# Segment attention with batch norm: the output stage takes its first four groups one at a time, and its matrix and vector operations in larger pieces

## The chip, the cores and the metric

The kernel runs on one core of a Trainium2 chip. The core's engines each work through their own queue: PE (TensorE, matrix products; its weight loads are shown apart as PEld), DVE (VectorE), ACT (ScalarE), POOL (GpSimd) and SP (SyncE, which here only issues transfers). Transfers are issued from the queues of SP, ACT and POOL and carried out by the core's 16 DMA engines. The metric is the device time of one execution in microseconds (us), lower is better. Times inside an execution are counted from the start of the span in the profile.

## The reference

There are N = 16384 tokens of D = 256 features and 8 segments. A token's segment is `bids`; its place in the segment is its index less the segment's start found by a binary search. Places are clamped to a padded table of 8 x 3072.

```python
q, k, v = feat @ Wq, feat @ Wk, feat @ Wv            # 32, 32 and 256 columns
starts = jnp.searchsorted(bids, jnp.arange(B))
pos = jnp.arange(N) - starts[bids]
qp, kp, vp = pad(q), pad(k), pad(v)                  # zeros(8, 3072, .).at[bids, pos].set(.)
scores = where(mask[:, None, :], einsum('bld,bmd->blm', qp, kp), -1e9)
rp = einsum('blm,bmd->bld', softmax(scores), vp)
t = rp[bids, pos] @ Wt
mu, var = t.mean(axis=0), t.var(axis=0)              # over all tokens
out = feat + relu((t - mu) / sqrt(var + 1e-5) * gamma + beta)
```

The mean and the variance need the `t` of all tokens, so nothing of the output can be finished before attention is over.

## The kernel before, in words

The segment ids of this input are not sorted, so most tokens' places fall outside their segment's table. Such a token reads one of 16 edge rows of the attention result (two per segment). Every other token has an attended row of its own: these are collected in lists, 48 tiles of 128 tokens (8 segments, 6 tiles each) in `tk`, with their features in `xs`, and a further list of 3 tiles, `L` with the features `xL`, whose rows are fetched by gathers (L836). A second, general path for other inputs (L41 to L530) isn't run here.

Attention is done segment by segment; the matrix products of L1008 and L953 fill PE. `statistics` (L1036) then forms mean, variance and scale, and the 16 finished edge rows after scale, shift and relu, split in three bf16 parts (48 rows), `y3` (L1062). It is complete at 255.35 us. What comes after is the output stage (L1405 to L1539), and it is where the change is made.

*Dense groups.* The tokens are 16 groups of 1024, each a tile of [128, 8, 256] f32 (1 MB). `ORDER` (L564) is the order in which they are treated: 0 to 6, then 15, 14, 13, 12, then 7 to 11. In this text d0 to d15 count in the order of treatment. For each group, PE multiplies a one-hot selection of edge rows `hot` by `y3` (L1483, one product per 128 tokens, 256 columns), the feature tile is added, and the tile goes to `out`. A group's parity decides which half of PE's rows it uses (rows 0 to 47 or 64 to 111), so the products of two groups of different parity can run at the same time.

*Pairs and iterations.* The groups are treated as eight pairs. A pair takes four iterations; each does two 128-token tiles of both groups, in accumulator tiles `pf` of 128x512 (one bank of the accumulator memory each; the pool `psF` has five). In the first two pairs DVE adds the features to the products (L1497), for both groups. From the third pair on it does so only for the first group of the pair; for the second, PE adds the features too, as a product with the identity matrix (L1488, f32, 256 columns, which is two passes on PE), and ACT copies the sum back into the tile (L1495).

*Buffers.* The feature tiles rotate through `IOB` = 6 buffers, `f_bufs`. Five lie in `work`, the memory of attention, and are loaded as soon as attention ends (L1083). The sixth, and then each buffer once its old group has been written, is loaded from SP's queue (L1473). The write of a group (L1501) is issued from ACT's queue after the pair, behind whatever copies ACT has in front of it.

*Rows.* `rows` (L1443) treats the listed tokens, two tiles at a time: on DVE multiply by `scale` (L1454), add `shift` (L1456), relu and add the features (L1458), with the intermediate `py` in accumulator memory (pool `psY`, two tiles of one bank). `scale` and `shift` come from three DVE operations behind the second pair (L1503 to L1505). `n_ops` says how many of these operations follow the additions of an iteration: none in pairs 0 and 1, 4 in 2 and 3, 3 later. `short_path_holds` (L1429) checks that no denominator has overflowed; it is called behind the fourth pair.

*Row writes.* POOL writes the finished rows to `out` with indirect transfers, one per tile, 51 in all (`put`, L1515, its transfer L1516). A listed token has also been written by its dense group, with a value that isn't its own; the row must come after that. So each write waits for dense groups, by an arm of a switch chosen from the segments' bounds (`ARMS`, L565). In this input the first six writes wait for d0 to d2, the next twelve for d0 to d4, eighteen for d0 to d6, and the last fifteen for d0 to d10 (12 tiles of `tk` and 3 of `L`).

What sets the order: DVE and PE follow the order of the Python loop, which is written out by hand (`manual_schedule`). ACT, SP and POOL are put in order by the framework's planner from its own estimates, so a group's write can stand behind copies of the next pair.

Of the kernel before, what the change touches and what calls it, by code (L numbers as in the profile page):

```python
# [18 lines left out]
P = 128  # L19
# [13 lines left out]
PART = 4  # L33
QA = TMIN * P
PB = 512
IOB = 6
LIM = 1.0e30


# [492 lines left out]
def segment_attention_bn_kernel(  # L532
# [44 lines left out]
    with ExitStack() as short:  # L577
# [828 lines left out]
        ahead = list(f_bufs)  # L1406
        while len(f_bufs) < IOB:
            f_bufs.append(io.tile([P, GT, D], F32, name=f"f{len(f_bufs)}"))
        fin = short.enter_context(tc.tile_pool(name="fin", bufs=1))
        psM = short.enter_context(tc.tile_pool(name="psM", bufs=1, space=PSUM))  # L1410
        psY = short.enter_context(tc.tile_pool(name="psY", bufs=2, space=PSUM))
        psF = short.enter_context(tc.tile_pool(name="psF", bufs=5, space=PSUM))
        out3 = out.rearrange("(g p i) d -> g p i d", p=P, i=GT)

# [9 lines left out]


        scale = psM.tile([P, 1, D], F32, name="scale")
        shift = fin.tile([P, 1, D], F32, name="shift")

        def short_path_holds():  # L1429

            lim = fin.tile([P, TT], F32, name="lim")
            nc.vector.tensor_scalar(lim, rdens, LIM, None, ALU.is_lt)
            good = fin.tile([P, TT], F32, name="good")
            odd = fin.tile([P, 1], F32, name="odd")
            nc.vector.scalar_tensor_tensor(
                good, rdens, 1.0 / LIM, lim, ALU.is_gt, ALU.mult, accum_out=odd
            )
            nc.vector.tensor_scalar(odd, odd, -1.0, float(TT), ALU.mult, ALU.add)
            ps_bad = psF.tile([P, 1], F32, tag="pf", name="ps_bad")
            nc.tensor.matmul(ps_bad, ones, odd, start=True, stop=True)  # L1440
            nc.vector.tensor_tensor(bad, ps_bad, over, ALU.add)

        def rows():  # L1443


            work = [(tk[:, ts(u, 2), :], xs[:, ts(u, 2), :]) for u in range(TT // 2)]
            for at in range(0, LT, 2):
                t = slice(at, min(at + 2, LT))
                work.append((L[:, t, :], xL[:, t, :]))
            for t, x in work:  # L1450
                T = t.shape[1]
                py = psY.tile([P, 2, D], F32, tag="py", name="py")
                p = py[:, 0:T, :]
                nc.vector.tensor_tensor(p, t, scale.to_broadcast([P, T, D]), ALU.mult)  # L1454
                yield
                nc.vector.tensor_tensor(p, p, shift.to_broadcast([P, T, D]), ALU.add)  # L1456
                yield
                nc.vector.scalar_tensor_tensor(t, p, 0.0, x, ALU.max, ALU.add)  # L1458
                yield
# [4 lines left out]
        dense = []  # L1464
        row = rows()

        pairs = [(k, k + 1) for k in range(0, NG, 2)]
        n_ops = [0, 0, 4, 4, 3, 3, 3, 3]
        with tc.manual_schedule(engines={mybir.EngineType.DVE, mybir.EngineType.PE}):
            for n, pair in enumerate(pairs):  # L1470
                for k in pair:
                    if k >= len(ahead):
                        nc.sync.dma_start(f_bufs[k % IOB], feat3[ORDER[k]])  # L1473
                for i in range(0, GT, 2):
                    pfs = {}
                    for k in pair:
                        pfs[k] = psF.tile([P, 2, D], F32, tag="pf", name=f"pf{ORDER[k]}")
                    for u in range(2):
                        for k in pair:
                            half, c = ORDER[k] % 2, ORDER[k] // 2  # L1480
                            r = slice(64 * half, 64 * half + 3 * NE)
                            on_pe = n > 1 and k % 2
                            nc.tensor.matmul(  # L1483
                                pfs[k][:, u, :], hot[r, c, i + u, :], y3[r, :],
                                start=True, stop=not on_pe,
                            )
                        if on_pe:
                            nc.tensor.matmul(  # L1488
                                pfs[k][:, u, :], ident, f_bufs[k % IOB][:, i + u, :],
                                start=False, stop=True,  # L1490
                            )
                    for k in pair:
                        two = f_bufs[k % IOB][:, i : i + 2, :]
                        if n > 1 and k % 2:
                            nc.scalar.copy(two, pfs[k])  # L1495
                        else:
                            nc.vector.tensor_add(two, two, pfs[k])  # L1497
                    for _ in range(n_ops[n]):
                        next(row, None)
                for k in pair:  # L1500
                    dense.append(nc.scalar.dma_start(out3[ORDER[k]], f_bufs[k % IOB]).ins)  # L1501
                if n == 1:
                    nc.vector.tensor_copy(scale[:, 0, :], scale_s)  # L1503
                    nc.vector.tensor_mul(shift[:, 0, :], mean, scale[:, 0, :])
                    nc.vector.tensor_sub(shift[:, 0, :], beta_bc, shift[:, 0, :])  # L1505
                if n == 3:
                    short_path_holds()
            for _ in row:
                pass
# [75 lines left out]
```

## Time and profile before

| what | us |
|---|---|
| median of 9 runs | 368.43 (364.29 to 369.02) |
| the profiled execution | 366.9 |
| its span | 365.0 |
| `y3` complete | 255.35 |
| write of d4 issued, landed | 282.04, 291.50 |
| last addition of d4 on DVE ends | 277.39 |
| write of d10 issued | 324.88 |
| last dense write landed | 353.74 |
| last row write starts, lands | 350.61, 354.72 |

Over the whole span PE is busy 288.9 us (79%), DVE 262.7 (72%), POOL 171.5 (47%) and ACT 109.3 (30%). In the output stage the dense writes take 7.2 / 8.0 / 9.7 us from issue to landing (minimum, median, maximum), and the loads of feature tiles 6.2 / 8.9 / 10.8. In one row of events the first number is the start in us, the second the length; then come engine, line and operation, the tiles written and read, and in square brackets the idle time of the engine just before, with what the profile holds to have ended it. In a table by stage, each engine has its busy time and number of instructions; then come the granted clock of PE as a share of full speed, the mean busy share of the DMA engines and what they moved in GB/s. In the list of waits each line has an engine, its tile and line, who released it, the time in total, how often, and the longest.

### The profile page before, as it was taken

How to read it: one execution, taken by the hardware profiler on the slowest of the kernel's cores; microseconds unless marked ns; L12 is line 12 of the kernel's file. 1: busy time of each engine (PE TensorE's matmuls, PEld its weight loads, DVE VectorE, ACT ScalarE, POOL GpSimd, SP SyncE). 2: the span in 40 equal slices, each digit the busy share in tenths (PEclk: the TensorE clock that was granted, in tenths of full speed). 3: DMA queues.
4: the chain of work that ended last, by engine and by line, in shares of the span. 5: the costliest groups of instructions: out<-in, count | busy, mean ns of one | idle time of the engine just before them, and what ended most of it. 6: DMA issues, size and time to landing. Idle time of an engine off the chain costs nothing. (4 is left out here: it accounts for less than half of the span.)

```text
span 365.0 us, 4145 instructions
## 1 busy us (share of the span) xinstructions
PE 288.9 (79%) x1139; PEld 178.5 (49%) x1139; DVE 262.7 (72%) x776; ACT 109.3 (30%) x208; POOL 171.5 (47%) x181
## 2 busy tenths in 40 slices
PE   1577599696899899399989999992896879999700
PEld 0335466473586488056865786661242334433200
DVE  7985399899798635488994356567998968888500
ACT  8525534233424441333222615430011102211100
POOL 3343353778782600477787710010305177776740
PEclk9998879898999999659999999997555555555555
DMA  4011111214013202211242010569699999996560
GB/s 114 24 32 30 38 56 33 66 39 139 0 49 123 70 9 63 62 48 44 72 127 69 10 59 29 177 216 370 262 392 381 407 398 379 351 407 263 201 234 3
DMA packets 20905, 53.34 MB, mean 146 GB/s; under 512 B 6606, under 2 KB 13344, under 8 KB 16746
## 3 DMA queue, kind: packets, MB, share of 16 engines
q1 hardware_dynamic: 11493, 25.06, 19.6%
q10 hardware_dynamic: 2421, 16.83, 11.2%
q0 software_dynamic: 6928, 10.81, 9.9%
q14 instruction: 48, 0.39, 0.4%
q8 instruction: 15, 0.25, 0.3%
HBM read 26.67 MB, written 29.92 MB: 155 GB/s over the span
## 5 line engine op out<-in xcount | busy, mean ns | idle before, releaser
L1008 PE MATMUL po<-work 128*128 128x257 f32 x394 | 100.5, 403 | 7.4 <-ACT work L972 4.4
L1008 PEld LDWEIGHTS po<-work 128*128 128x128 f32 x394 | 76.6, 201 | 23.9 <-ACT work L972 7.5
L836 POOL DMA_INDIRECT xs<-in_r_feat,idx x48 | 52.7, 1099 | 50.3 <-issue 27.6
L1516 POOL DMA_INDIRECT out<-tk,idx x48 | 47.3, 985 | 37.3 <-DVE py L1454 15.3
L836 POOL DMA_INDIRECT reads_r<-reads_of,idx x48 | 53.6, 1116 | 20.2 <-issue 14.7
L1488 PE MATMUL pf<-work,ident 128*128 128x256 f32 x64 | 39.1, 714 | 3.0 <-DMA work<-in_r_feat 3.0
L953 PE MATMUL pv<-wvt,work 128*128 128x256 f32 x164 | 37.9, 383 | 1.2 <-ACT work L945 1.0
L972 ACT ACTIVATE work<-s,mask 128x512 f32<-128x512 f32 (+2 forms) x62 | 32.6, 601 | 13.3 <-PE s L967 10.8
L953 PEld LDWEIGHTS pv<-wvt,work 128*128 128x128 f32 x164 | 30.6, 190 | 8.7 <-ACT work L945 3.0
L1483 PE MATMUL pf<-y,hot 48*128 48x256 bf16 x128 | 27.0, 391 | 9.8 <-DVE y L1062 7.1
L1497 DVE TENSOR_TENSOR work<-work,pf 128x512 f32<-128x512 f32 x40 | 26.1, 682 | 10.9 <-PE pf L1483 10.9
L997 ACT ACTIVATE sq<-tk 128x256 f32<-128x256 f32 x39 | 16.3, 417 | 55.4 <-DVE tk L1013 51.1
L1483 PEld LDWEIGHTS <-hot 48*128 48x128 bf16 x128 | 7.0, 104 | 43.4 <-issue 43.3
L967 PE MATMUL s<-work 32*128 32x512 f32 (+2 forms) x124 | 25.9, 607 | 2.7 <-ACT work L972 2.7
L1012 DVE RECIPROCAL rdens<-po 128x1 f32<-128x1 f32 x39 | 6.1, 160 | 26.6 <-PE po L1008 26.5
L922 PE MATMUL px<-ident,xs 128*128 128x128 f32 x82 | 17.5, 319 | 7.9 <-issue 2.6
L1495 ACT COPY work<-pf 128x512 f32<-128x512 f32 x16 | 9.4, 586 | 47.6 <-PE pf L1488 47.6
L934 PE MATMUL pqk<-work,wqk 128*128 128x512 f32 (+2 forms) x52 | 21.9, 561 | 0.2 <-ACT work L927 0.2
L1488 PEld LDWEIGHTS pf<-work,ident 128*128 128x128 f32 x64 | 16.0, 310 | 12.4 <-issue 9.1
L922 PEld LDWEIGHTS px<-ident,xs 128*128 128x128 f32 x82 | 10.7, 159 | 19.3 <-issue 6.6
L957 ACT COPY work<-pv 128x512 f32<-128x512 f32 (+1 forms) x21 | 12.1, 576 | 25.8 <-PE pv L953 25.8
L1488 PE MATMUL pf<-f,ident 128*128 128x256 f32 x32 | 19.5, 714 | 0.0
(241 smaller groups left out, 380.9 us busy)
## 6 DMA issues: line engine op xcount, KB each, us to landing
work<-in_r_feat SPq DMA_DIRECT2D x14, 1024.0 KB, 8.4
out<-work ACTq DMA_DIRECT2D x14, 1024.0 KB, 7.9
t_rows<-tk SPq DMA_DIRECT2D x3, 768.0 KB, 3.9
t_rows<-tk SPq DMA_DIRECT2D x4, 512.0 KB, 5.0
f<-in_r_feat SPq DMA_DIRECT2D x2, 1024.0 KB, 6.2
out<-f ACTq DMA_DIRECT2D x2, 1024.0 KB, 8.5
eb<-edge_of SPq DMA_DIRECT2D x16, 96.0 KB, 2.4
t_rows<-tk SPq DMA_DIRECT2D x4, 256.0 KB, 3.1
```

The costliest lines, as they stand in the source:

```text
L836: nc.gpsimd.indirect_dma_start(out=dst, out_offset=None, in_=table, in_offset=bass.IndirectOffsetOnAxis(ap=ind, axis=0), bounds_check=n - ...
L922: nc.tensor.transpose(px[:, ts(t, P)], xs[:, b * FT + t0 + t, ts(h, P)], ident)
L934: nc.tensor.matmul(pqk[:, 0:w], wqk[:, h, :], xT[:, h, own_c], start=(h == 0), stop=(h == DH - 1),)
L953: nc.tensor.matmul(pv[:, t, :], xT[:, h, ts(t0 + t, P)], wvt[:, h, :], start=(h == 0), stop=(h == DH - 1),)
L967: nc.tensor.matmul(s[:, i, 0:w], k[g, t // 4, :], q[g, c : c + w], start=True, stop=True)
L972: nc.scalar.activation((pr_b if c else pr_a)[:, t, 0:w], s[:, i, 0:w], AF.Exp, bias=mask[:, m : m + 1],)
L997: nc.scalar.activation(sq, tk[:, at, :], AF.Square)
L1008: nc.tensor.matmul(po, pr[:, t, ts(r, P)], v[:, t, :], start=(t == 0), stop=(t == T - 1))
L1483: nc.tensor.matmul(pfs[k][:, u, :], hot[r, c, i + u, :], y3[r, :], start=True, stop=not on_pe,)
L1488: nc.tensor.matmul(pfs[k][:, u, :], ident, f_bufs[k % IOB][:, i + u, :], start=False, stop=True,)
L1497: nc.vector.tensor_add(two, two, pfs[k])
L1516: w = nc.gpsimd.indirect_dma_start(out=out, out_offset=bass.IndirectOffsetOnAxis(ap=idx[:, at : at + 1], axis=0), in_=y, in_offset=None, b ...
```

## The change

- The first four groups are treated one by one; the other twelve as six pairs. All additions of the first four stay on DVE, as before.
- `scale` and `shift` are computed behind the third group (d2), and the first unit of rows follows at once; the second unit follows behind d3.
- In a pair, the identity product takes 512 columns (both tiles of an iteration) and comes first; the one-hot products are then added to it.
- Rows go four tiles at a time (128x1024; the 3 tiles of `L` in one piece), so there are 13 units of three operations instead of 26. `py` is one tile of two banks instead of two of one. `n_ops` becomes 2 in the first two pairs and 1 later.
- There are seven feature buffers instead of six. To make room, `shift` and the small tiles of `short_path_holds` move into `late`, memory that `statistics` has finished with. `short_path_holds` is called behind the second pair, (6, 7).

```diff
@@ -33,7 +33,7 @@
 PART = 4
 QA = TMIN * P
 PB = 512
-IOB = 6
+IOB = 7
 LIM = 1.0e30
 
 
@@ -1406,9 +1406,8 @@
         ahead = list(f_bufs)
         while len(f_bufs) < IOB:
             f_bufs.append(io.tile([P, GT, D], F32, name=f"f{len(f_bufs)}"))
-        fin = short.enter_context(tc.tile_pool(name="fin", bufs=1))
         psM = short.enter_context(tc.tile_pool(name="psM", bufs=1, space=PSUM))
-        psY = short.enter_context(tc.tile_pool(name="psY", bufs=2, space=PSUM))
+        psY = short.enter_context(tc.tile_pool(name="psY", bufs=1, space=PSUM))
         psF = short.enter_context(tc.tile_pool(name="psF", bufs=5, space=PSUM))
         out3 = out.rearrange("(g p i) d -> g p i d", p=P, i=GT)
 
@@ -1424,14 +1423,14 @@
 
 
         scale = psM.tile([P, 1, D], F32, name="scale")
-        shift = fin.tile([P, 1, D], F32, name="shift")
+        left = late.rearrange("p t m -> p (t m)")
+        shift = left[:, 0:D].unsqueeze(1)
 
         def short_path_holds():
 
-            lim = fin.tile([P, TT], F32, name="lim")
+            lim, good = (left[:, D + i * TT : D + (i + 1) * TT] for i in range(2))
+            odd = left[:, D + 2 * TT : D + 2 * TT + 1]
             nc.vector.tensor_scalar(lim, rdens, LIM, None, ALU.is_lt)
-            good = fin.tile([P, TT], F32, name="good")
-            odd = fin.tile([P, 1], F32, name="odd")
             nc.vector.scalar_tensor_tensor(
                 good, rdens, 1.0 / LIM, lim, ALU.is_gt, ALU.mult, accum_out=odd
             )
@@ -1443,13 +1442,10 @@
         def rows():
 
 
-            work = [(tk[:, ts(u, 2), :], xs[:, ts(u, 2), :]) for u in range(TT // 2)]
-            for at in range(0, LT, 2):
-                t = slice(at, min(at + 2, LT))
-                work.append((L[:, t, :], xL[:, t, :]))
-            for t, x in work:
+            work = [(tk[:, ts(u, 4), :], xs[:, ts(u, 4), :]) for u in range(TT // 4)]
+            for t, x in [*work, (L, xL)]:
                 T = t.shape[1]
-                py = psY.tile([P, 2, D], F32, tag="py", name="py")
+                py = psY.tile([P, 4, D], F32, tag="py", name="py")
                 p = py[:, 0:T, :]
                 nc.vector.tensor_tensor(p, t, scale.to_broadcast([P, T, D]), ALU.mult)
                 yield
@@ -1464,46 +1460,54 @@
         dense = []
         row = rows()
 
-        pairs = [(k, k + 1) for k in range(0, NG, 2)]
-        n_ops = [0, 0, 4, 4, 3, 3, 3, 3]
+
+
+        steps = [(0,), (1,), (2,), (3,), (4, 5), (6, 7), (8, 9), (10, 11), (12, 13), (14, 15)]
+        n_ops = [0, 0, 0, 0, 2, 2, 1, 1, 1, 1]
+
+        def feats(k):
+            if k >= len(ahead):
+                nc.sync.dma_start(f_bufs[k % IOB], feat3[ORDER[k]])
+
         with tc.manual_schedule(engines={mybir.EngineType.DVE, mybir.EngineType.PE}):
-            for n, pair in enumerate(pairs):
-                for k in pair:
-                    if k >= len(ahead):
-                        nc.sync.dma_start(f_bufs[k % IOB], feat3[ORDER[k]])
+            for n, step in enumerate(steps):
+                for k in step:
+                    feats(k)
                 for i in range(0, GT, 2):
                     pfs = {}
-                    for k in pair:
+                    for k in step:
                         pfs[k] = psF.tile([P, 2, D], F32, tag="pf", name=f"pf{ORDER[k]}")
+                        if k != step[0]:
+                            nc.tensor.matmul(
+                                pfs[k], ident, f_bufs[k % IOB][:, i : i + 2, :],
+                                start=True, stop=False,
+                            )
                     for u in range(2):
-                        for k in pair:
+                        for k in step:
                             half, c = ORDER[k] % 2, ORDER[k] // 2
                             r = slice(64 * half, 64 * half + 3 * NE)
-                            on_pe = n > 1 and k % 2
                             nc.tensor.matmul(
                                 pfs[k][:, u, :], hot[r, c, i + u, :], y3[r, :],
-                                start=True, stop=not on_pe,
+                                start=(k == step[0]), stop=(k == step[0] or u == 1),
                             )
-                        if on_pe:
-                            nc.tensor.matmul(
-                                pfs[k][:, u, :], ident, f_bufs[k % IOB][:, i + u, :],
-                                start=False, stop=True,
-                            )
-                    for k in pair:
+                    for k in step:
                         two = f_bufs[k % IOB][:, i : i + 2, :]
-                        if n > 1 and k % 2:
+                        if k != step[0]:
                             nc.scalar.copy(two, pfs[k])
                         else:
                             nc.vector.tensor_add(two, two, pfs[k])
                     for _ in range(n_ops[n]):
                         next(row, None)
-                for k in pair:
+                for k in step:
                     dense.append(nc.scalar.dma_start(out3[ORDER[k]], f_bufs[k % IOB]).ins)
-                if n == 1:
+                if n == 2:
                     nc.vector.tensor_copy(scale[:, 0, :], scale_s)
                     nc.vector.tensor_mul(shift[:, 0, :], mean, scale[:, 0, :])
                     nc.vector.tensor_sub(shift[:, 0, :], beta_bc, shift[:, 0, :])
-                if n == 3:
+                if n in (2, 3):
+                    for _ in range(3):
+                        next(row)
+                if n == 5:
                     short_path_holds()
             for _ in row:
                 pass
```

## The prediction, made before the changed kernel was run

> **What bounds the kernel now.** I read the end first and went backwards. The chain that ended last has only four pieces, all in the last 16 us: POOL's writes of rows, L1516. So the next question is what released that queue, and I read POOL's own row of events (start, length, in square brackets the idle time before and what the profile blames):
>
> ```profile
> span 365.0 us, 4145 instructions
> PEclk9998879898999999659999999997555555555555
> 282.04 0.34 ACTq L1501 DMA_DIRECT2D out<-work  x1
> ...
> 292.36 0.99 POOL L1516 DMA_INDIRECT out<-tk,idx  x1 [8.37 <-DVE py L1456]
> 293.65 0.98 POOL L1516 DMA_INDIRECT out<-tk,idx  x1 [0.30 <-issue]
> ...
> 332.57 0.98 POOL L1516 DMA_INDIRECT out<-tk,idx  x1 [1.82 <-DVE py L1454]
> ...
> 350.61 0.99 POOL L1516 DMA_INDIRECT out<-L,idx  x1 [0.30 <-issue]
> ```
>
> There are 51 row writes. Six run at 275.77 to 284.0. Then POOL idles 8.37 us; from 292.36 a write starts every 1.29 (0.98 and 0.30), with one further wait of 1.82, which is 1.52 over the usual 0.30. The check: 44 steps x 1.29 = 56.76; 292.36 + 56.76 + 1.52 = 350.64, and the last one starts at 350.61. So the end is the start of this second batch, plus that extra wait, plus a fixed chain. The vector operations named in the brackets were long done: the 8.37 ends 0.86 after the write of the fifth dense group (d4, counted from 0 in order of treatment) landed at 291.50, and the wait at 332.57 ends about as long after the eleventh (d10, issued 324.88) landed. After the last start come 4.1 us to its landing (354.72) and 10.3 of closing work.
>
> Why does d4 land so late? Its last addition ended at 277.39, but on ACT its write stands behind a copy that waits for PE, which waited for the load of the next odd group:
>
> ```profile
> 279.24 1.22 PE L1488 MATMUL pf<-work,ident 128*128 128x256 f32 x2 [3.01 <-DMA work<-in_r_feat]
> 281.98 0.59 ACT L1495 COPY work<-pf 128x512 f32<-128x512 f32 x1 [5.45 <-PE pf L1488]
> ...
> core 0: us, PE busy (x) PEld busy (x) DVE busy (x) ACT busy (x) POOL busy (x), PEclk, DMA share, GB/s
> 255.50:266.00 10.50, 8.89 (x39) 2.83 (x40) 9.89 (x17) 0.00 (x0) 3.03 (x3) 0.50 0.71 281
> 266.00:279.00 13.00, 10.23 (x28) 4.04 (x28) 12.66 (x22) 2.35 (x4) 2.03 (x2) 0.50 1.00 395
> 279.00:294.00 15.00, 11.58 (x30) 4.74 (x30) 13.95 (x23) 2.34 (x4) 5.26 (x6) 0.50 0.99 382
> 294.00:345.00 51.00, 49.00 (x130) 19.88 (x130) 39.91 (x67) 9.07 (x16) 37.90 (x39) 0.50 0.88 338
> ...
> DVE work L1497 <- PE pf L1483: 10.9, 18, 1.6
> ```
>
> The table by stage says two more things. PE is busy 49.00 of 51.00 us after 294 and DVE waits 10.9 us for it, at a granted clock of 0.50 throughout. And DMA is full (1.00, 0.99) while d4 is on its way. Yet all of PE's work ends before the row writes do: the last dense write lands at 353.74, 1.0 before the last row. So after 292 PE has little to give: it can only take away the 1.52 for d10 and about a microsecond of crowding at the end. The price of the change is set before 292.
>
> **The change part by part** (times from the start of the span; the profiled execution took 366.9: span 365.0 and 1.9 around it. That is 1.5 below the median of 368.43 of the nine runs; I work out a difference and add it to the median.)
>
> *First four groups one by one, seventh buffer.* The 16 first additions stay on DVE. Before, they ran pair by pair, 0.60 apart, 256.11 to 265.65. Now d0, d1, d2 need 4 each and finish at about 258.6, 261.0, 263.4 (before: writes issued 260.42, 261.01, 265.20). Nothing is added; d2, on which the first six row writes wait, leaves 1.8 earlier. These six end the batch 2 to 3 us earlier, which is hidden: POOL then waits for d4 either way. The seventh buffer is one 1 MB load at 251 instead of later on SP's queue; it runs where DMA share is 0.71 and takes the load of the second odd group out of 268.39 to 279.20. With that, PE's 3.01 wait goes.
>
> *Rows four tiles at a time, scale and first two units pulled forward.* An operation of 128x512 takes 682 to 698 ns; the nearest rows for 128x1024 f32 are other vector operations on this chip at 1203 to 1229 (L1111, L1112, L1125). 39 operations of about 1.25 (dependent) or 1.13 (overlapped) replace 78 of 0.72 or 0.60: some 4 to 5 us of DVE saved over the stage, but DVE was not the bound after 294. What matters is the order at the start: scale and shift (three of 0.42) end at 264.7, unit 0 (3 x 1.25) at 268.4, the four additions of d3 at 270.9, unit 1 at 274.6. Then come the additions of d4 with two row operations between them: 0.60 + 1.25 + 1.13 = 2.98 per step, the fourth ends at 274.6 + 3 x 2.98 + 0.69 = 284.2. Before, d4 was added up at 277.39: **this part moves d4 back by 6.8 us on DVE**, of which the next paragraph shows how much was waiting anyway. Working with one accumulator tile instead of two makes a unit's first operation wait for the last one of the unit before, but both are DVE's own, in order.
>
> *Identity products of 512 columns.* Before, an iteration (two tiles of both groups of a pair) took 2.96 on PE: four identity passes of 0.575 (0.59 and 0.56) and two pairs of one-hot products at 0.33. Now: two passes of 512. Back-to-back f32 products of 257 columns at the half clock were 0.427 apart in the attention stage (158.8 to 162.4), so 512 columns are 0.853 of streaming; if the 0.148 by which the tail's passes exceed that stays with each pass, 1.00. Lower bound 2 x 0.853 + 0.66 = 2.37, upper 2 x 1.00 + 0.66 = 2.66 (and 2.96 if nothing is gained). I take 2.53, between them, since the second weight load can hide behind a longer pass.
>
> *When d4 leaves.* In the changed kernel's order on ACT, d4's write stands behind the third copy of the following pair (before: behind the first). PE's first identity is free at 264, but its iteration is completed by the one-hot product whose accumulator bank comes free with the first addition of d3 at 269.3: iteration 1 ends at 270.0. Six more of 2.53 end at 285.2; the seventh uses the bank that ACT copies out of only after the sixth, 0.8 more: 286.0. So the write goes at **286.1, against 282.04: 4.1 later**. By 2.37 it is 285.1 (DVE's 284.2 is the floor), by 2.66 it is 286.9, by 2.96 it is 288.7.
>
> *When it lands.* Before, 9.46 (282.04 to 291.50), together with two loads, d5's write and row writes. Now the first row writes are over and the load of the odd group is not there, so it shares with one load and d5's tail: nearest is d6 before, issued 291.47 beside a load at 291.57, landed after 7.23. The writes' minimum is 7.2, their median 8.0; almost alone in the beginning it was 4.65. I take 7.2: 293.3, and the second batch starts 0.87 later at **294.2, against 292.36: +1.8**. Bounds 285.1 + 6.8 (2 MB at the 395 GB/s of 266 to 279 is 5.3, and 1.5 of the first write's 4.65 for being under way) and 286.9 + 9.46, each + 0.87: 292.8 to 297.2.
>
> *What is late next.* d10: its write must land before the 31st step, 294.2 + 30 x 1.29 = 332.9. PE takes two of four pairs at 2.53 and the other at DVE's 2.98, so it leaves at 321 (before 324.88), lands at 329: **the 1.52 goes**. d6 (in the case of this input the 13th write of the batch waits for it: 294.2 + 12 x 1.29 = 309.7) leaves after pair two at some 298 and lands by 307: not late, by 2.7 us. The row units: the last ends with PE's last iteration, about 341 to 342, 6 us before the first L row. Nothing else waits. At the end the dense write is over some 3 us earlier than 353.74, so the last row lands in 3.5 to 4.1 instead of 4.1: 0 to -0.6.
>
> *The sum.* +1.8 (second batch) - 1.52 (d10) - 0.3 (last landing) = 0.0. The profiled execution would stay at 366.9, the median at 368.4. With the bounds: a batch at 292.8 gives +0.4 - 1.52 - 0.6 = -1.7, one at 297.2 gives +4.8 - 1.52 - 0 = +3.3.
>
> **Weighing a rule: PE's clock.** The tail before kept 0.50 although PE is busy 0.96 of 294 to 345: busy is not streaming. Per iteration 4 x 0.427 + 2 x 0.21 = 2.13 of 2.96 stream, 0.72; of 2.53 it would be 0.84, and in the attention stage, with products back to back, the clock row shows 9s. At full clock PE's iteration would halve; then DVE's 284.2 holds d4, it leaves at 284.4, lands at 291.2 to 291.6, the batch starts at 292.1 to 292.5.
> The Trainium skill, "TensorE: Matmul & The Clock Gate", Part 1, says that the throttled state is the default and one busy window of about 3.4 us releases it. Read simply, that rule would have freed the clock before, where the row shows 0.50 for 110 us; so the trace asks for a denser window than the page's word "busy" gives, and no row says if 0.84 is enough. By the rule the sum would be -1.7 to -2.2, by the row 0.0.
>
> **The rivals.**
> *Clock rises (faster).* As above: 292.3 + 56.76 = 349.1, 1.5 less than 350.61, less 0.3 to 0.6 at the end, and up to 1 more if d4's landing meets emptier queues: -1.8 to -3, 365.4 to 366.6. For it: 0.84 against 0.72; against: DVE-paced iterations (2.98) fall back to 0.71.
> *d4 lands as slowly as before (slower).* DMA was at 0.99, and the same megabytes pass; 286.1 + 9.46 + 0.87 = 296.4, last write at 353.2: +2.3 to +2.6, 371; with iterations of 2.96 +5, 373. It decides when the second batch starts after 292.36 + 1.52 + 1.84 = 295.7.
> *The change gains nothing on PE and hides all the same.* Iterations of 2.96 but a landing of 7.2: 288.7 + 7.2 + 0.87 = 296.8, +2.6. It joins the case above.
> *The first batch's row writes or d6 hold the queue:* d6 only if it leaves after 301; unlikely, +1 to +2.
>
> **How the numbers follow.** Even chain 0.44 (its own range 366.8 to 370.0), clock 0.26, late d4 0.26, other small waits 0.04. "Within 0.5%" is 1.84 us, about what a measurement of this kernel can tell from no change. The even case gives 0.28 within, 0.08 faster, 0.08 slower; clock 0.21 faster, 0.05 within; late d4 0.23 slower, 0.03 within; the rest 0.02 on each side. Together faster 0.31, within 0.36, slower 0.33. For 8 in 10 the range takes in the clock's full -3 and late d4 to +3.3: 365.2 to 371.7.
>
> **What would show it.** Right: d4's write issued at 285 to 287 behind a copy, POOL's long wait ending at 293 to 295, no second wait near 332, last row at 350 to 351.5; identity passes of 0.85 to 1.0; vector operations of 1024 at 1.2 to 1.25; granted clock 0.50 in the tail. Wrong: a clock above 0.5 after 265, an issue after 288, a landing above 9, a second long wait on POOL, or row writes farther apart than 1.29.

## The result, and the profile after

The changed kernel takes 364.03 us (median of 16 runs, 360.25 to 366.52) against 367.63 (53 runs of before): a ratio of 0.9883 with a 95% interval of 0.986 to 0.9906. It is 1.2% faster. I had forecast no change, with a range from 365.2 up: wrong, and on the side of the rival in which PE's clock rises. The profiled execution took 364.68, span 362.9.

The page of the changed kernel, its head, and the row of the granted clock in tenths over 40 slices:

```profile
span 362.9 us, 4009 instructions
PE 257.6 (71%) x1091; PEld 161.6 (45%) x1091; DVE 257.3 (71%) x737; ACT 109.2 (30%) x208; POOL 172.1 (47%) x181
PEclk9996989898799999959999999999557757985855
```

Before, the clock row ended in twelve fives. Now there are sevens, eights and a nine among them. The table by stage, with the stages of the prediction (the columns are busy time and number of instructions by engine, then granted clock, DMA share and GB/s):

```profile
255.50:266.00 10.50, 9.24 (x34) 3.76 (x34) 9.60 (x19) 0.00 (x0) 3.03 (x3) 0.50 1.02 424
266.00:279.00 13.00, 9.41 (x29) 2.52 (x28) 12.83 (x15) 2.45 (x5) 3.77 (x4) 0.60 0.99 389
279.00:294.00 15.00, 4.42 (x18) 1.32 (x18) 14.83 (x16) 2.23 (x4) 2.56 (x4) 0.75 1.01 408
294.00:340.00 46.00, 27.28 (x98) 8.17 (x98) 31.62 (x40) 8.80 (x15) 35.05 (x36) 0.75 0.90 341
```

PE's busy time from 279 to 294 fell from 11.58 to 4.42: it is no longer what DVE waits for there. DVE is busy 14.83 of 15.00, so DVE now holds d4. The events of ACT around d4's write, and POOL's row writes:

```profile
282.69 0.59 ACT L1496 COPY work<-pf 128x512 f32<-128x512 f32 x1 [1.57 <-PE pf L1489]
284.98 0.34 ACTq L1502 DMA_DIRECT2D out<-work  x1
...
273.63 1.03 POOL L1520 DMA_INDIRECT out<-tk,idx  x1 [8.37 <-DVE py L1450]
...
293.63 0.98 POOL L1520 DMA_INDIRECT out<-tk,idx  x1 [11.83 <-DMA out<-work]
...
332.53 0.98 POOL L1520 DMA_INDIRECT out<-tk,idx  x1 [0.55 <-issue]
...
350.57 0.98 POOL L1520 DMA_INDIRECT out<-L,idx  x1 [0.30 <-issue]
```

d4 leaves at 284.98, 0.03 after its last addition (284.27 + 0.68 on DVE); the copy ahead of it in the line of ACT was done 1.7 earlier (282.69 + 0.59). The long wait before the second batch is still there (11.83; before 8.37), the 1.82 before the 37th write (the first that needs d10) has shrunk to 0.55.

In this execution the edge rows `y3` were complete at 256.38, 1.03 later than in the profile of before. The code ahead of them is the same. The changed kernel without its row writes (below) has 256.51, two other kernels 254.77 and 255.29; whether the later start is chance, these five profiles can't say. I count from there:

| from `y3` on, us | before | forecast | after |
|---|---|---|---|
| d4's write issued | 26.69 | 30.75 | 28.60 |
| issue to landing of d4 | 9.46 | 7.2 | 7.85 |
| second batch of row writes starts | 37.01 | 38.85 | 37.25 |
| extra wait before the 37th row write | 1.52 | 0 | 0.24 |
| last row write starts | 95.26 | 95.6 | 94.19 |
| its landing takes | 4.11 | 3.8 | 2.22 |
| closing work | 10.28 | 10.28 | 10.11 |
| end of span | 109.65 | 109.7 | 106.52 |

The stage is 3.13 us shorter. Against the forecast, 1.6 of it is the second batch (DVE instead of PE holds d4) and 1.6 the landing of the last row write. Against before, the second batch is no gain (0.24 later): 1.28 come from the wait for d10, 1.89 from the last landing and 0.17 from the closing work.

### The profile page after: what moved, and what is told of

The parts are those of the page before. It is cut to its first block, busy times and chain, and to the rows that moved or that the text cites. A ratio compares the mean times of both kernels' runs of the same rounds, so it can differ in the third digit from the quotient of the medians.

```text
span 362.9 us, 4009 instructions
## 1 busy us (share of the span) xinstructions
PE 257.6 (71%) x1091; PEld 161.6 (45%) x1091; DVE 257.3 (71%) x737; ACT 109.2 (30%) x208; POOL 172.1 (47%) x181
## 4 chain that ended last, share of the span: by engine, by line
PE 40%; DVE 39%; issue 8%; DMA 4%; POOL 3%; ACT 2%; DVEq 0%; ACTq 0%; POOLq 0%
PE po L1008 19%; PE pv L953 7%; DVE work L1498 4%; PE s L967 4%; DVE py L1450 4%; PE pqk L934 4%; DVE py L1452 4%; DMA out<-tk,idx 3%; POOL out L1520 3%; PE px L922 3%; DVE tk L1454 3%; DVE tk L1013 2%; DVE work L941 2%; DVE oh L850 2%; DVE acc L998 1%
## 5 line engine op out<-in xcount | busy, mean ns | idle before, releaser
L1008 PEld LDWEIGHTS po<-work 128*128 128x128 f32 x394 | 75.7, 199 | 26.4 <-ACT work L972 7.5
L1498 DVE TENSOR_TENSOR work<-work,pf 128x512 f32<-128x512 f32 x32 | 20.6, 679 | 14.3 <-issue 10.4
L1481 PE MATMUL pf<-work,ident 128*128 128x512 f32 x32 | 21.7, 767 | 12.6 <-DMA work<-in_r_feat 10.2
L1489 PE MATMUL pf<-y,hot 48*128 48x256 bf16 x128 | 18.5, 329 | 11.8 <-DVE y L1062 7.1
L922 PE MATMUL px<-ident,xs 128*128 128x128 f32 x82 | 16.7, 310 | 9.1 <-ACT work L945 3.7
L934 PE MATMUL pqk<-work,wqk 128*128 128x512 f32 (+2 forms) x52 | 20.6, 533 | 0.4 <-ACT work L927 0.4
L993 DVE SCALAR_TENSOR_TENSOR acc<-tk,reads_r,acc 128x256 f32<-128x256 f32 x39 | 18.7, 479 | 0.9
L1013 DVE SCALAR_TENSOR_TENSOR tk<-po,rdens,sref 128x256 f32<-128x256 f32 x39 | 18.7, 481 | 0.9
```

The lines of the kernel that those rows point to most:

```text
L922: nc.tensor.transpose(px[:, ts(t, P)], xs[:, b * FT + t0 + t, ts(h, P)], ident)
L934: nc.tensor.matmul(pqk[:, 0:w], wqk[:, h, :], xT[:, h, own_c], start=(h == 0), stop=(h == DH - 1),)
L1008: nc.tensor.matmul(po, pr[:, t, ts(r, P)], v[:, t, :], start=(t == 0), stop=(t == T - 1))
L1013: nc.vector.scalar_tensor_tensor(tk[:, at, :], po[:, 0:D], rdens[:, one], sref, ALU.mult, ALU.subtract)
L1481: nc.tensor.matmul(pfs[k], ident, f_bufs[k % IOB][:, i : i + 2, :], start=True, stop=False,)
L1489: nc.tensor.matmul(pfs[k][:, u, :], hot[r, c, i + u, :], y3[r, :], start=(k == step[0]), stop=(k == step[0] or u == 1),)
```

## The experiments

Two theories. **Clock:** with the identity product first, PE streams densely enough that its clock is granted in full, and that carries the gain. **Order and buffers:** the gain comes from the first groups one by one and the seventh buffer, and the clock is beside the point.

A remark that all but the runs without row writes need: they landed on chips on which the kernel before takes 403 to 409 us (medians) instead of 368. Its own trace there is shown below. Ratios are always against runs of before on the same chip. In the profiles from there `y3` is complete anywhere between 279.1 and 294.2 us, in code that is the same in all of them; that spread is wider than what the change is worth. So I add, where it helps, how long the profiled execution took from `y3` to the end of its span: 120.5 us for before, 118.7 and 119.1 for two profiles of the changed kernel. These are single executions.

### One part undone, one part alone

The identity product of 512 columns put into the kernel before, and nothing else:

```diff
+on_pe = n > 1
+if on_pe:
+    k = pair[1]
+    nc.tensor.matmul(pfs[k], ident, f_bufs[k % IOB][:, i : i + 2, :], start=True, stop=False)
 for u in range(2):
     for k in pair:
...
-        nc.tensor.matmul(pfs[k][:, u, :], hot[r, c, i + u, :], y3[r, :], start=True, stop=not on_pe)
+        mix = on_pe and k % 2
+        nc.tensor.matmul(pfs[k][:, u, :], hot[r, c, i + u, :], y3[r, :], start=not mix, stop=(not mix or u == 1))
-    if on_pe:
-        nc.tensor.matmul(pfs[k][:, u, :], ident, f_bufs[k % IOB][:, i + u, :], start=False, stop=True)
```

> The kernel before with one part of the change: in the pairs, the identity product takes 512 columns and comes first. Clock theory: PE's iteration streams more densely, the granted clock rises to full in part of the stage after 268 us, d10 leaves earlier and the second long wait of the row writes (1.52) goes, the last dense write ends earlier: 1.5 to 2.5 us faster than before. Rival (the order of the first groups and the seventh buffer make the gain, the clock is beside the point): within 0.7 us of before.

Measured: 0.9944 (0.9903 to 0.9985), a median of 409.23 against 409.45; the clock row of the output stage has sevens and eights again. So the clock rises with this part alone. The time doesn't decide: by the ratio it is 0.6% (2.3 us of 409), as the clock theory said, but the interval goes from 0.6 to 4.0 us, and the medians differ by 0.2, as the rival said.

The reverse, the changed kernel with the products of before:

```diff
-if k != step[0]:
-    nc.tensor.matmul(pfs[k], ident, f_bufs[k % IOB][:, i : i + 2, :], start=True, stop=False)
 for u in range(2):
...
+    if len(step) > 1:
+        nc.tensor.matmul(pfs[k][:, u, :], ident, f_bufs[k % IOB][:, i + u, :], start=False, stop=True)
```

> The changed kernel with the identity products of before (256 columns, behind the one-hot product). Clock theory: granted clock 0.50 through the whole output stage, PE's iteration 2.96, d4 leaves at 288 to 289 instead of 285, the second batch of row writes starts at 296 to 298: 3 to 6 us slower than the changed kernel, so 367 to 370. Rival (order and buffers make the gain): within 1 us of the changed kernel's 364.

> The changed kernel with identity products of 256 columns, again, now beside the changed kernel on one chip. Clock theory: clock 0.50 throughout, d4 leaves 3 to 4 us later, the whole 2 to 3 per cent slower than the changed kernel and 1 to 2 per cent slower than before. Rival (order and buffers make the gain): within 0.4 per cent of the changed kernel.

> The changed kernel with identity products of 256 columns behind the one-hot products, once more on another chip. As before: clock 0.50 in the whole output stage, 1.5 to 2 per cent slower than the kernel before.

Measured: 1.0161 (1.0112 to 1.021), 1.0211 (1.0143 to 1.0278) and 1.0142 (1.0049 to 1.0234) of before, on three chips. The granted clock is 0.50 through the whole output stage in each. From `y3` to the end the first and the third took 124.2 and 126.9, against 118.7 and 119.1 for the changed kernel. On the chip of the second, the changed kernel itself stood beside it:

> The changed kernel itself, beside the others on one chip. Clock theory: granted clock above 0.5 in parts of the output stage from about 272 us on, 1 to 1.6 per cent faster than before, as on record.

Measured for the changed kernel: 1.0005 (0.9955 to 1.0055). So there its gain over before was gone, against what I expected; but 2.1% lie between it and the version with the old products. The rival's "within 0.4 per cent of the changed kernel" falls: with everything else of the change in place, the order of PE's products is worth 2%.

The order of the first groups alone (with 256 columns, rows two tiles at a time, six buffers):

```diff
-pairs = [(k, k + 1) for k in range(0, NG, 2)]
-n_ops = [0, 0, 4, 4, 3, 3, 3, 3]
+steps = [(0,), (1,), (2,), (3,), (4, 5), (6, 7), (8, 9), (10, 11), (12, 13), (14, 15)]
+n_ops = [0, 0, 0, 0, 4, 4, 2, 2, 2, 2]
...
-if n == 1:
+if n == 2:
     nc.vector.tensor_copy(scale[:, 0, :], scale_s)
...
+if n in (2, 3):
+    for _ in range(6):
+        next(row)
```

> The kernel before with one part of the change: the first four groups one by one, first rows behind the third and fourth; identity products of 256 columns, rows two tiles at a time, six buffers as before. Clock theory: clock 0.50, d4 held back on DVE to about 285 and by PE to 288, the second batch at 296 to 298, d10 in time: 2 to 5 us slower than before. Rival (the order makes the gain): 1 to 4 us faster than before.

Measured: 1.0187 (1.0124 to 1.025), clock 0.50. In its profile, of an execution of 425.7 us, the second batch starts 41.7 us after `y3` (335.93 less 294.23), against 37.5 for the kernel before on such a chip. The order of the groups, with the rows brought forward, costs time when it is alone: 7.7 us by the ratio, more than I had said; its rival expected a gain.

The changed kernel with `IOB = 6`:

> The changed kernel with six feature buffers. Clock theory: DVE holds d4 at 285 either way, the load of the seventh group comes later and PE waits for it, which costs 0 to 1.5 us. Rival (the seventh buffer carries the gain): 2 to 4 us slower than the changed kernel.

Measured: 0.9871 (0.9811 to 0.993) of before; the changed kernel wasn't on that chip. On two others of the kind it stood at 1.0005 and 1.0089, so nothing says that the seventh buffer is worth anything there. d4's write leaves 28.6 after `y3`, as it does with seven.

The changed kernel with rows two tiles at a time (`psY` with two one-bank tiles, `n_ops` doubled):

> The changed kernel with rows two tiles at a time (twice as many operations behind each iteration, two one-bank accumulator tiles). Clock theory: DVE needs 6 operations of 0.65 to 0.72 for what now takes 3 of 1.25, some 0.4 us more per unit; d4's last addition comes about 1.5 later, so 1 to 2 us slower than the changed kernel; the clock rises as it does there. Rival (the larger row operations carry the gain): 3 us slower or more, no gain left over before.

Measured: a median of 410.78 of 12 runs, beside 408.61 for the changed kernel and 408.81 for before; no ratio with an interval could be formed. The 2.2 us are close to the expectation but settle nothing. In its profile d4's write leaves 30.3 after `y3` instead of 28.6, about the 1.5 later that was expected, and the clock rises.

### The width, or the order of the products?

The changed kernel with identity products of 256 columns, but both first and in a row:

```diff
-nc.tensor.matmul(pfs[k], ident, f_bufs[k % IOB][:, i : i + 2, :], start=True, stop=False)
+for u in range(2):
+    nc.tensor.matmul(pfs[k][:, u, :], ident, f_bufs[k % IOB][:, i + u, :], start=(u == 0), stop=False)
```

> The changed kernel with identity products of 256 columns that come first, both tiles of an iteration in a row, then the four one-hot products. Does the width of 512 release the clock, or the order alone? If the width: each pass keeps its 0.15 us over the streaming, the iteration is 2.8 to 2.96, clock 0.50, like the kernel with 256 behind the one-hot products. If the order: passes 0.43 apart, iteration 2.5, the clock rises, within 0.5 per cent of the changed kernel.

By time it is unclear: 1.0103 (1.0038 to 1.0167) of before, from five runs of 399.4 to 406.49, with no changed kernel beside it. From `y3` to the end its profile took 116.5, a little less than the changed kernel's. The trace is clear on the clock. PE's events in the changed kernel, in this one, then in the one with 256 columns behind the one-hot products (its third run), all at half clock but for the last row of the first, in which the clock rises:

```profile
270.57 2.08 PE L1481 MATMUL pf<-f,ident 128*128 128x512 f32 x2
272.58 0.61 PE L1489 MATMUL pf<-y,hot 48*128 48x256 bf16 x4
273.11 2.07 PE L1481 MATMUL pf<-f,ident 128*128 128x512 f32 x2
275.66 1.46 PE L1481 MATMUL pf<-f,ident 128*128 128x512 f32 x2
```

```profile
298.71 2.07 PE L1482 MATMUL pf<-f,ident 128*128 128x256 f32 x4
300.72 0.61 PE L1490 MATMUL pf<-y,hot 48*128 48x256 bf16 x4
301.26 2.07 PE L1482 MATMUL pf<-f,ident 128*128 128x256 f32 x4
303.26 0.61 PE L1490 MATMUL pf<-y,hot 48*128 48x256 bf16 x4
```

```profile
295.97 1.22 PE L1489 MATMUL pf<-f,ident 128*128 128x256 f32 x2
297.12 0.40 PE L1484 MATMUL pf<-y,hot 48*128 48x256 bf16 x2
297.45 1.22 PE L1489 MATMUL pf<-f,ident 128*128 128x256 f32 x2
298.60 0.40 PE L1484 MATMUL pf<-y,hot 48*128 48x256 bf16 x2
```

Four passes in a row start 2.55 apart from the next four (298.71 to 301.26), with the one-hot products between: the same iteration as with 512 columns (270.57 to 273.11, 2.54). Cut in two by one-hot products, an iteration is 2 x 1.48 = 2.96. And the clock follows, in the tables by stage of the two:

```profile
298.00:306.00 8.00, 7.88 (x29) 4.06 (x28) 7.90 (x10) 1.76 (x3) 2.03 (x2) 0.54 0.96 366
306.00:314.00 8.00, 5.80 (x34) 3.23 (x32) 7.93 (x9) 2.75 (x5) 3.94 (x4) 1.00 1.02 424
```

```profile
293.00:301.00 8.00, 8.00 (x23) 3.53 (x22) 7.90 (x9) 1.17 (x2) 2.86 (x3) 0.50 0.99 374
301.00:309.00 8.00, 7.65 (x21) 3.01 (x20) 7.90 (x10) 1.75 (x3) 3.10 (x4) 0.50 0.88 295
```

PE is busy 8.00 of 8.00 in the kernel that stays at 0.50, and 7.88 in the one that goes to 1.00. So it is the order, not the width of 512. Whether it matters that the identity products come first or only that they stand in a row, no run separates.

### What the order of the products is worth to the dense groups alone

The last three kernels leave out the 51 row writes of POOL (listed tokens keep their dense group's value); the rows are still computed. They ran together, on a chip where before takes 367.04 (the record numbers it 10, like the chip on which before took 408.81 in an earlier batch; if that is the same chip, the slowness is a matter of time and not of the chip):

```diff
-for arm in tc.Switch({mybir.EngineType.Pool: which}, len(ARMS)):
...
-            put(tk[:, at, :], at, waits[b])
-    for t in range(LT):
-        put(L[:, t, :], TT + t, max(waits.values()))
```

> The kernel before without the 51 row writes of POOL (the listed tokens keep their dense group's value). If late increments in the output stage come from the row writes' own completions, they are gone here even on a chip that has them: d10's write leaves about 69 us after the edge rows, the last dense write about 90, as in the profile of before, and the clock stays 0.50. If they come from elsewhere, d10 still leaves at 80 or later.

> The changed kernel without the row writes. The dense chain alone, with the clock rising: d4's write leaves 28 to 29 us after the edge rows (before 26.7), d10's at 58 to 60 (before 69.5), the last at 80 to 85 (before 90.4).

> The changed kernel with identity products of 256 columns behind the one-hot products, without the row writes. Clock theory: 0.50 throughout, d4 at 31 to 33, d10 at 68 to 72, the last at 94 to 100: what the clock is worth to the dense chain is the difference to the run without row writes of the changed kernel, about 10 us at d10.

| without row writes | before | changed | changed, 256 columns behind |
|---|---|---|---|
| median of 2 runs | 357.40 | 348.73 | 361.69 |
| of before with row writes | 0.9738 (0.9649 to 0.9826) | 0.9501 (0.941 to 0.9593) | 0.9854 (0.9776 to 0.9933) |
| d4's write after `y3` | 26.10 | 28.61 | 32.15 |
| d10's | 68.94 | 60.62 | 68.50 |
| the last | 89.85 | 79.04 | 92.18 |

The stage from 294 to 345 in the three, in this order:

```profile
294.00:345.00 51.00, 48.98 (x130) 19.83 (x130) 39.51 (x63) 9.38 (x16) 0.00 (x0) 0.50 0.61 244
```

```profile
294.00:345.00 51.00, 28.34 (x98) 8.27 (x98) 34.58 (x44) 9.38 (x16) 0.00 (x0) 0.73 0.72 280
```

```profile
294.00:345.00 51.00, 46.62 (x128) 19.39 (x128) 31.42 (x39) 8.91 (x16) 0.00 (x0) 0.50 0.60 242
```

The changed kernel with its products is 13.0 us faster than with those of before (361.69 to 348.73), and d10 leaves 7.9 earlier, where about 10 was expected. (d4's times are within what was expected; d10 of the changed kernel is 0.6 later than that, the last writes of the two are 1 to 2 us earlier.) These 13.0 us are the clock and the shorter iterations together. At half clock an iteration of 2.54 in place of 2.96 saves at most 24 x 0.42 = 10.1 us over the six pairs, so at least 2.9 are the clock's own, an estimate from these rows. How the rest divides isn't shown, since no kernel had the new order at a clock that stayed at 0.50. The order without the dense products is 4.3 slower than before. So the dense chain is 8.7 us faster by the change (357.40 to 348.73), and 3.6 (medians) to 4.3 (ratio) reach the end with row writes. There POOL's chain sets the end, and its second batch, which can't start before d4 lands, starts no earlier than before. Whether late increments (next section) come from the row writes was asked too; this chip had none in any of the three, so that stays open.

### Where the gain goes on the slower chips

> The kernel before itself, with its profile, on a chip of the kind that the experiments ran on (there it takes 400 to 409 us instead of 368). If the increments of PE's semaphore come late there at about 77 to 105, 233 and 340 to 367 us, as in all the other kernels' traces from such chips, that is the chip's and not the change's: long waits of ACT and DVE for products that had long ended, at the same places.

> The changed kernel beside it. On a chip with such late increments: the second batch of row writes starts as in its profile (about 37 us after the edge rows), but d10's write leaves 10 us or more later than there and the row writes wait for it, so the gain at the end is lost: within 0.5 per cent of before. On a chip without them: 1 to 1.5 per cent faster.

Measured: before itself against the other runs of before 0.9962 (0.9921 to 1.0004), which shows how far two samples of one kernel lie apart there; the changed kernel 1.0089 (1.0023 to 1.0155) of before. The medians are 407.48 for before, 409.1 for the other runs of before and 407.71 for the changed kernel, so neither a gain nor a loss is shown. In the two profiles `y3` is 3.2 later in the changed kernel (288.45 and 285.21), and what comes after is 1.8 shorter (118.7 and 120.5).

The kernel before on such a chip, one event of ACT in the attention stage, then two waits of its row writes, the 31st and the 37th:

```profile
99.36 0.59 ACT L957 COPY work<-pv 128x512 f32<-128x512 f32 x1 [19.67 <-remote]
...
358.26 0.98 POOL L1516 DMA_INDIRECT out<-tk,idx  x1 [4.88 <-DVE tk L1458]
371.05 0.98 POOL L1516 DMA_INDIRECT out<-tk,idx  x1 [4.96 <-DVE tk L1458]
```

And the changed kernel beside it:

```profile
326.08 0.98 POOL L1520 DMA_INDIRECT out<-tk,idx  x1 [12.37 <-DMA out<-work]
362.86 0.69 DVE L1498 TENSOR_TENSOR work<-work,pf 128x512 f32<-128x512 f32 x1 [11.53 <-remote]
376.78 0.98 POOL L1520 DMA_INDIRECT out<-tk,idx  x1 [12.35 <-DVE f L1498]
```

"remote" is the profile's word where it found no releaser. Both instructions wait for PE's semaphore alone, and the last product that PE had done had ended 17.6 and 12.0 us before. Such waits, for products that ended up to 23.5 us before, lie between 82 and 107 us and between 335 and 380 in all fifteen traces from these chips, and most have one between 229 and 245 too. In the five from chips at 368 there is no wait of over 2 us that the profile calls remote. The second batch starts 37.6 after `y3`, as in the record (37.25). But d10's write leaves 82.5 after `y3` (59.4 in the record) and the row writes wait 12.35 for it; before waits 4.96 there, d10 leaving at 81.2. (Its 4.88 is another wait: the 31st write needs rows that DVE, held up by such a product, finishes only at 357.98.) With both kernels held at the same point, the earlier d10 is gone, and the last row write starts 106.4 after `y3` in the changed kernel and 103.9 in before. From `y3` on, before ends later all the same, because its last dense write is issued 106.9 after `y3` (96.7 in the changed kernel) and moves data until 398.9, after all its row writes. What delays the increments of PE's semaphore on those chips isn't known.

### Where the rest of the wait can be had

If POOL's wait for d4 is what is left, d4 should be treated sooner: five groups one by one, and the first rows only behind the fifth.

```diff
-steps = [(0,), (1,), (2,), (3,), (4, 5), (6, 7), (8, 9), (10, 11), (12, 13), (14, 15)]
-n_ops = [0, 0, 0, 0, 2, 2, 1, 1, 1, 1]
+steps = [(0,), (1,), (2,), (3,), (4,), (5, 6), (7, 8), (9, 10), (11, 12), (13, 14), (15,)]
+n_ops = [0, 0, 0, 0, 0, 2, 2, 2, 2, 1, 0]
-if n == 2:
+if n == 4:
     nc.vector.tensor_copy(scale[:, 0, :], scale_s)
...
-if n in (2, 3):
-    for _ in range(3):
+if n == 4:
+    for _ in range(6):
         next(row)
```

> The changed kernel with the first five groups one by one, scale, shift and two units of rows behind the fifth, the others as pairs (5,6) to (13,14) and the last alone. If the row writes' idle time before the second batch (11.8 us in the changed kernel) is what is left on the path: d4 leaves at about 270 instead of 285, the first batch starts at about 274.5 as now, the second follows without a gap, and the end comes 3 to 8 us earlier than in the changed kernel. If the transfers are the limit (DMA share 0.99 to 1.02 from 255 to 294): 0 to 2 us.

> First five groups one by one, rows behind the fifth, again on another chip: 2 to 3 per cent faster than before; the second batch of row writes follows the first with a gap under 4 us.

Measured: 0.9724 (0.9638 to 0.9811) and 0.9691 (0.9606 to 0.9777) of before. The wait before the second batch is 2.15 and 2.75. A second version has `n_ops` 2, 2, 1, 2, 1, 1 from the fifth group on:

> The same with one row operation instead of two behind each iteration of the pair (9,10), and two behind those of (11,12): d10 is added up 5 us earlier, so its write lands earlier and the third batch of row writes waits less; 0 to 3 us faster than the version with two operations everywhere. If transfers set the end: no difference beyond 0.5 us.

> First five groups one by one, one row operation behind each iteration of (9,10): 2.5 to 4 per cent faster than before on either kind of chip, since the gap before the second batch goes (from 11 to 3.5 us).

Measured: 0.9609 (0.9489 to 0.9729) and 0.9699 (0.9581 to 0.9818). On the chip where both versions ran, the second had a median of 390.22 against 393.84, but the intervals overlap: not told apart. POOL in the second version's second run:

```profile
301.07 1.02 POOL L1520 DMA_INDIRECT out<-tk,idx  x1 [10.62 <-DVE tk L1454]
...
307.73 0.98 POOL L1520 DMA_INDIRECT out<-tk,idx  x1 [0.30 <-issue]
311.08 0.98 POOL L1520 DMA_INDIRECT out<-tk,idx  x1 [2.37 <-DMA out<-work]
```

The first row write starts 18.0 after `y3` (301.07 less 283.06), the second batch 28.0 instead of 37.6: the wait of 12.37 is 2.37. From `y3` to the end the four profiles took 106.8 to 113.0 (changed kernel 118.7 and 119.1). These versions beat before on the three chips that they ran on, and the changed kernel on the two where it ran too (398.65 to 408.61, 396.68 to 407.71). None of them ran on a chip at 368.

## Why the prediction was wrong

*The chain that sets the end: right.* In the two profiles at 368, the row writes after d4 are the end of both kernels. Starting from the measured second batch, 44 steps of 1.29 and the small wait give 293.63 + 56.76 + 0.24 = 350.63; measured 350.57.

*d4 moved back on DVE: right.* Forecast 284.2 (28.85 after `y3`), measured 284.95 (28.57). Row operations of 128x1024 took 1.22 to 1.23 where I had 1.25, and 0.60 + 1.25 + 1.13 = 2.98 was 2.99 to 3.00 (275.29, 278.28, 281.27, 284.27).

*The iteration of PE: right at half clock, by luck.* 2.53 forecast, 2.54 measured, from two errors that cancel: the two passes took 2.01 (270.57 to 272.58), which was my upper bound (2.53 leaves 1.87 for them), and the one-hot products 0.53 instead of 0.66. The reason I gave, longer passes, wasn't it: passes of 256 columns do the same when they stand in a row.

*The clock: the step that failed.* I wrote that no row says if a streaming share of 0.84 is enough, and then took 0.50 as the likeliest, with 0.44 against 0.26. It rose at about 276, after two whole iterations of 2.54 (270.57 to 275.66). The rival's path was right in place (DVE's end of the additions holds d4) and right in the second batch: 36.75 to 37.15 after `y3` forecast there, 37.25 measured. I could have read it from the profile of before. With an f32 column at 0.427/257 us at half clock and half that at full, bf16 columns at half of it, and products that run at the same time counted once, one can add up the streaming in each 3.4 us window of the clock's record, an estimate from these rows. In the attention stage of before, the clock rises at 33.3, 50.3, 70.8, 91.3 and 163.0 us, after windows of 0.84, 1.00, 0.87, 0.93 and 1.00 (one of 0.87 passed without). In the output stage of the traces with the interleaved order no window goes over 0.76, but for one of 0.80, and the clock never rises. In those with the identity product first, it rises after windows of 0.81 to 0.87 (one of 0.79), though some of up to 0.83 passed without. The 0.84 that I had worked out stood in that range.
The Trainium skill, "TensorE: Matmul & The Clock Gate", Part 1, has the gate open after one busy window of about 3.4 us. The runs agree once "busy" is read as streaming: PE at 8.00 of 8.00 busy stayed at 0.50 in the trace above.

*The last landing: mis-sized.* I gave 0 to 0.6; it was 1.9 (4.11 to 2.22). The last dense write is issued 341.39 instead of 345.79, and the trace's last dense packet ends at 349.3 instead of 353.3. In the same trace a row write of 341.56, among dense writes, took 8.0 to land, one of 348.00 took 3.5, and the last 2.2. In before, one of 341.59, between two dense writes, took 2.4. That the emptier queues do it is read from these rows, not shown by a run.

*d10: right.* Of the 1.52 before the 37th write, 1.28 went. The 0.24 that stayed is hardly d10's, whose write had left 16.7 us before. It left 59.4 after `y3`, against 321 forecast, or 65.7. The 65.7 was for iterations of 2.53 at half clock, so I put the 6.3 between them down to the clock; no run shows the clock alone.

*The slower rival* (landing 9.46) didn't come: 7.85, between my 7.2 and the median of 8.0.

*The range.* Its lower end, 365.2, was the rival's 365.4 at full clock; measured 364.0. The rival was short by the last landing, 1.3 more than the 0.6 it was allowed. My base, 368.43, also lay 0.8 above the 367.63 of the 53 runs.

## What to carry to other kernels

When PE is "busy" all the time and its clock still reads 0.50, look at the order of its products: here, products with other operands between two halves of the same work cost 0.42 us of an iteration of 2.96, and the clock too. Before costing a change at the old clock, add up its streaming per window and compare with the windows of the same trace in which the clock did rise. And a chain that becomes 8.7 us faster gives only what the next wait lets through: here 3.6 to 4.3, since another engine's writes wait for one early group. Bringing that group forward as well gave 2.8 to 3.9% over before on the slower chips, where the change alone showed no gain.

## What was not expected of the hardware

- Four f32 identity passes of 256 columns take as long in a row (2.55 an iteration) as two of 512 (2.54); with one-hot products between them, 2.96, in every kernel that had them so.
- The clock went up and down several times within the stage: 0.60 from 266 to 279, 0.75 from 279 to 340, with each rise after a dense stretch and each fall after PE had waited. In the dense chain alone, this and the shorter iterations were worth 13.0 us.
- On some chips (or at some times) ACT and DVE saw the end of a PE product up to 23.5 us late, in the same stretches in every kernel. The kernel before takes 35 to 41 us more there, and one and the same change read 0.988 on one kind of chip and 1.000 to 1.009 on the other.
